# Spacing of the gathers, pieces per step and the distance of the query fold in a two-layer perceiver kernel

## The chip, the cores and the metric

The kernel runs on one core of a Trainium2 chip. The metric is the device time of one execution in microseconds (us). The engines are named as the profile names them: PE multiplies matrices (PEld is its weight load), DVE, ACT and POOL work on vectors, SP issues most of the transfers (DMA). ACT and POOL issue some too.

## What is computed

The input is 16 batches of 64 latent rows of 256 values, in float32, and a context of 16 x 1601 x 256. Two layers follow each other, each with three parts, and each part adds to the latents `x`:

```
x = x + L0_xattn(ctx, ctx, norm(x), mask)   # 16 heads; each query reads 5 places of the context per head
x = x + L0_attn(norm(x))                    # sigmoid attention inside a batch
x = x + L0_ffn(norm(x))                     # 8 experts, the best 2 per row
x = x + L1_xattn(norm(x), ctx)              # 16 heads of 64; 77 text rows and 1524 image rows, two softmaxes
x = x + L1_attn(norm(x))                    # a state space layer
x = x + L1_ffn(norm(x))                     # 32 experts, the best 4 per row, and shared ones
```

In the first cross attention keys and values of all context rows are projected, and each query then reads, for each head and each of five sampling places, two neighbouring rows and weighs them:

```
i0 = floor(ix); w0 = 1 - dx; w1 = dx
sk = 0.5 * (w0 * gather(K, i0) + w1 * gather(K, i0 + 1))      # the same for sv with V
ctx = softmax(Q . sk / sqrt(16)) . sv
```

## The kernel before, in words

The 1024 latent rows are eight tiles of 128 rows (two batches to a tile), kept on the chip in `x4`. PE, DVE and ACT run in an order written out by hand in the code (`manual_schedule`, so their instructions stand as the program issues them). The instructions of POOL and SP are placed by the framework, which may put a load ahead of its place in the code.

**Keys and values** (`keys_values`, lines 364 to 411). A loop over `s` from 0 to 112 makes one step of it each time: seven steps per batch. A step transposes up to two chunks of 128 context rows (`cx`, L153), and projects the chunks of the span before (`st<-wkv,cxt`, L88) into `kv`, which ACT copies out of the accumulators (L382) and writes to a table in memory (`tab<-kv`). `texts` (from step 18) prepares the text part of the second layer's cross attention beside it.

**Gathers and attends.** For each tile and each four heads there is a unit, 32 in all, four per tile. `gather(k)` issues half a unit: a copy of ten columns of indices on DVE (`ig`, L427) and ten indirect transfers on POOL (`g<-tab,ig`, L429); `ig` and `g` have four buffers each. `attend(i)` computes one unit's attention on DVE, in two halves with an exponential on ACT in the first (L449 to L481); it writes `cv`. When these are issued is decided by `tick(us)`, called at many places with a fixed number that stands for the time gone by. It keeps a sum, `now`. A gather is issued at the first call at which `now` has reached `pace["gather"]`, as long as it is less than four units ahead of the attends, and it sets the next time `APART` later, or `APART_X` once cross attention exists (`cr`). A unit's two halves may be issued from `AFTER` (42) on after its last gather. At most one gather and one half are issued in a call. The loop calls `tick(3.9)` in each step from step 0, `tick(2.4)` more while the texts run, and gathers are open from step 14.

**The first tiles' part.** At step 60 the text pools are closed and a pool `lp` is opened for tiles 0 and 1, then tile 2: their attention (`attention`) and dense experts (`middle`, eight experts of four pieces, three weight loads of 512 KB to an expert into four buffers `w`). Tile 3's attention (`late`) goes with them. `mid` issues one piece, if enough units are attended (8 for tiles 0 and 1, 12 for tile 2, 16 for tile 3), and calls `tick(2.4)` for it, and `tick(1.0)` for a piece of `late`:

```
        def mid():

            if mids and attended() >= mids[0][0]:
                if next(mids[0][1], True) is None:
                    tick(2.4)
                else:
                    mids.pop(0)
            if len(mids) < 2 and attended() >= 4 * (ND0 + 1) and next(late, True) is None:
                tick(1.0)
```

What is left of them when the keys and values are done is issued alone, in a loop `while mids`, before cross attention begins.

**Cross attention of the second layer** (`Cross`). `begin` loads text keys and values (`kt`, `vt`), weights (`wk`, `wq`), makes the queries of tile 0, turns the first batch's context (`cn`, `turn`) and folds the first queries. Then 131 steps follow, one for each of 16 batches times 8 pairs of heads, and three to end. Step `n` takes the folded query `qf` of its pair, multiplies it with the context in three groups (`st<-qf,cT`, L88), each in one of four accumulator banks `st`; DVE takes the maximum of each group (`mp`, L1090), PE turns it (L1109), DVE reduces it (`xmx`, L1111), PE spreads it (L1119), ACT copies it (`mc`, L1121). DVE subtracts it from the groups (`pt`, L1130) and ACT takes exponentials. In the same step PE multiplies the `pt` of step n-1 with the context (L1059, three parts), and finishes step n-2 (`turn_out`, `out`). `fold` multiplies the key weights with a query (L1015), and ACT copies the result into `qf` (L1018). A step calls `tick(5.2)` three times.

Steps run without side work until all 32 units are attended. Then a side chain (attention and routed experts of tiles 3 to 7) runs along, up to five pieces a step, as long as the step is below 42; what is left of it is drained alone. Then come three groups of the state space layer and the routing of the last part (`Ssm.group`, `Route.group`); group g begins when step 32 g + 35 is reached and runs on as side pieces of the steps. The last group and the experts of the second layer follow from about 3000 us on.

In `Ssm.group` the normalized rows are the tile `mn`, their transposes `mt`, the product of input and step width `dx`, and the output sum `y` (the tile `ys`), each with one buffer of 128 x 2 x 256 values.

Of the kernel before, what the change touches and what calls it, by code (L numbers as in the profile page):

```python
# [17 lines left out]
P = 128  # L18
B, S, D = 16, 64, 256
M = 1601  # L20
KC = D // P
# [3 lines left out]
NS = H0 * NK  # L25
LEFT = -NK // 2
HU = 4
APART, APART_X, AFTER = 16.0, 12.0, 42.0
RP = 4


# [34 lines left out]
def perceiver_kernel(ctx: ExitStack, tc: tile.TileContext, a: dict, out: bass.AP):  # L66
    nc = tc.nc

    def mk(pool, shape, tag, dtype=F32, bufs=None):
        return pool.tile(list(shape), dtype, tag=tag, name=tag, bufs=bufs)  # L70
# [836 lines left out]
    class Cross:  # L907
# [98 lines left out]
        def fold(self, n):  # L1006

            if n >= B * NHP:
                return
            b, hp = divmod(n, NHP)  # L1010
            w = self.w[b, hp // 4]
            rhs = qbds[b // 2 % 2][:, hp, b % 2].rearrange("p h q -> p (h q)")
            pf = bank()
            for k in range(KC):
                nc.tensor.matmul(pf[:, k * P : (k + 1) * P], lhsT=w[:, hp % 4, k * P : (k + 1) * P], rhs=rhs,  # L1015
                                 start=True, stop=True)
            qf = self.qf[n] = mk(self.xp, [P, KC, P], "qf", bufs=2)
            nc.scalar.copy(qf.rearrange("p c n -> p (c n)"), pf[:, : KC * P])  # L1018

        def out(self, n):  # L1020
# [49 lines left out]
        def step(self, side=None, mid=None, more=None, late=None):  # L1070

            n = self.n
            b, hp = divmod(n, NHP)
            t, bb = divmod(b, 2)
            last = B * NHP
            live = n < last
            old = 0 <= n - 1 < last
            if live:
                ct, qf = self.ctx[b], self.qf.pop(n)
                mp_ = mk(self.xp, [P, NB, P], "mp", bufs=1)  # L1080
                st = []
            for i in range(NB):
                if live:
                    s = big().rearrange("p (c n) -> p c n", n=P)
                    for c in range(4):
                        j = (i * 4 + c) * P
                        mm(s[:, c, :], [(ct[:, k, j : j + P], qf[:, k, :]) for k in range(KC)])
                    st.append(s)
                if live:
                    nc.vector.tensor_reduce(mp_[:, i, :], s.rearrange("p c n -> p n c"), AX.X, ALU.max)  # L1090
                    if i:
                        nc.vector.tensor_tensor(mp_[:, 0, :], mp_[:, 0, :], mp_[:, i, :], ALU.max)
                if i == 1 and n - 2 < last:
                    self.turn_out(n - 2)
                if i == 1 and more is not None:
                    next(more, None)
                if i == 0:
                    tick(5.2)
            if n - 2 < last:
                self.out(n - 2)  # L1100
            if hp == NHP - 1:
                self.turn(b + 1)
            if old:
                po = bank()[:, : D + 1]
                self.product(n - 1, 0, po)
            if live:

                tm = bank()
                nc.tensor.transpose(tm[:, :P], mp_[:, 0, :], ident)  # L1109
                mx = mk(small, [P, 1], "xmx")  # L1110
                nc.vector.tensor_reduce(mx, tm[:, :P], AX.X, ALU.max)  # L1111
            if mid is not None:
                next(mid, None)
            tick(5.2)
            if old:
                self.product(n - 1, 1, po)
            if live:
                mb = bank()
                nc.tensor.transpose(mb[:, :P], mx.to_broadcast([P, P]), ident)  # L1119
                mc = mk(self.xp, [P, P], "mc", bufs=1)  # L1120
                nc.scalar.copy(mc, mb[:, :P])  # L1121
                mc = mc.unsqueeze(1)
            self.fold(n + 1)
            if live:
                pt = pts[n % 2]
                for i in range(NB):
                    c0 = i * 4
                    m = 4 if i + 1 < NB else 3
                    o = pt[:, c0 : c0 + m, :]
                    nc.vector.tensor_tensor(o, st[i][:, :m, :], mc.to_broadcast([P, m, P]), ALU.subtract)  # L1130
                    nc.scalar.activation(o, o, AF.Exp)  # L1131
                o = pt[:CR, CM, :]
                nc.vector.tensor_tensor(o, st[-1][:CR, 3, :], mc[:CR, 0, :], ALU.subtract)
                nc.scalar.activation(o, o, AF.Exp)
            if late is not None:
                next(late, None)
            if old:
                self.product(n - 1, 2, po)
                rc = mk(small, [P, 1], "xrc")
                nc.vector.reciprocal(rc, po[:, D:])  # L1140
                os_ = self.os[n - 1] = mk(self.xp, [P, D], "os", bufs=1)
                nc.vector.tensor_scalar(os_, po[:, :D], rc, None, ALU.mult)

            if hp == 0:
                self.weights(b, 1)
                self.text_loads(b + 1)
            if hp == 1 and b >= 1:
                self.loads(b + 1)
            if hp == 4:
                self.weights(b + 1, 0)  # L1150
            if bb == 1 and hp in (2, 3, 4):
                self.queries(t + 1, hp - 2)
            if hp == 5:
                self.text(b + 1, 0)
            elif hp == 6:
                self.text(b + 1, 1)
                self.text_turn(b + 1, 0)
            elif hp == 7:
                self.text_turn(b + 1, 1)
            if bb == 0 and hp == 2:  # L1160
                self.project(t - 1)
            if side is not None:
                next(side, None)
            tick(5.2)
            self.n += 1

        def begin(self, xp):
            self.xp = xp
            self.text_loads(0)
            self.weights(0, 0)  # L1170
            yield
            for part in range(3):
                self.queries(0, part)
                yield
            self.turn(0)
            self.loads(1)
            yield
            self.text(0, 0)
            yield
            self.text(0, 1)  # L1180
            self.text_turn(0, 0)
            yield
            self.text_turn(0, 1)
            self.fold(0)
            yield


# [4 lines left out]
    class Ssm:  # L1192
# [15 lines left out]
        def group(self, g, wide=None):  # L1208

            mp, w_in, w_xp, w_out, cw, cb, dp, al = (  # L1210
                self.mp, self.w_in, self.w_xp, self.w_out, self.cw, self.cb, self.dp, self.al)
            tiles = range(g * TG, (g + 1) * TG)
            sh = [P, KC, TOK]
# [59 lines left out]
            nc.vector.tensor_scalar(dt, dt, 0.0, None, ALU.max)  # L1273
            nc.vector.scalar_tensor_tensor(dt, q_, 2.0, dt, ALU.mult, ALU.add)
            yield
            dx = mk(mp, sh, "dx")
            y = mk(mp, sh, "ys")
            nc.vector.tensor_tensor(dx, xc, dt.unsqueeze(1).to_broadcast(sh), ALU.mult)
            for c in range(KC):
                nc.vector.tensor_scalar(y[:, c, :], xc[:, c, :], dp[:, c : c + 1], None, ALU.mult)  # L1280
# [223 lines left out]
    cr = None  # L1504
# [6 lines left out]
    def tick(us):  # L1511

        pace["now"] += us
        now = pace["now"]
        k = pace["k"]
        if pace["open"] and now >= pace["gather"] and k < 2 * len(units) and k // 2 < attended() + 4:
            gather(k)
            pace["due"][k // 2] = now + AFTER
            pace["k"] = k + 1
            pace["gather"] = now + (APART if cr is None else APART_X)  # L1520
        i = attended()
        if i < len(units) and pace["k"] > 2 * i + 1 and now >= pace["due"][i]:
            next(attends)
            pace["sub"] += 1

    ET = mybir.EngineType
    with tc.manual_schedule(engines={ET.PE, ET.DVE, ET.Activation}):
# [25 lines left out]
        for s in range(B * 7 + 1):  # L1553
            run(kv)
            if s >= 1:
                run(early)
            if s == 14:
                pace["open"] = True
            tick(3.9)
            if s >= 18 and next(text, True) is None:  # L1560
                tick(2.4)
            if s == 60:
                drain(text)
                stx.close()
                tc.swap_default_side()
                slp = ExitStack()
                lp = slp.enter_context(tc.tile_pool(name="lp", bufs=2))
                tc.swap_default_side()
                mw = Middle(lp)
                for t0, nt in ((0, TG), (TG, ND0 - TG)):  # L1570
                    mids += [(4 * (t0 + nt), attention(t0, nt, lp, mw)), (0, middle(t0, nt, lp, mw))]
                late = attention(ND0, 1, lp, mw)
                for k in range(KC):
                    nc.vector.tensor_scalar(rws[:, k, :], rws[:, k, :], rsc[:, k : k + 1], None, ALU.mult)
            if lp:
                mid()
        drain(kv)
        skv.close()
# [2 lines left out]
        cr = Cross(xc)  # L1581
# [161 lines left out]
```

## Time and profile before

| | us |
|---|---|
| median of 3 runs | 3313.22 (3308.72 to 3315.46) |
| time of the profiled execution | 3307.06 |
| its span, first to last instruction | 3305.1 |
| PE busy in the span | 2924.7 |
| DVE, ACT, POOL busy | 1620.0, 1026.4, 818.2 |
| mean granted clock of PE | 0.946 |

The span is that of the instructions in one profiled execution; 2 us lie around it. An engine is busy while it executes; waiting, branching and issuing of transfers do not count. The clock is the share of full speed that the throttle granted to PE. In the tables of time windows each row has the window and its length, then the busy time of each engine with the number of instructions in brackets, then the clock, the mean busy share of the 16 DMA engines, and what they moved in GB/s. A row of waits names the engine and what it wanted to do, after the arrow what ended the wait, then us in total, the number of waits, and the longest.

### The profile page before, as it was taken

What the parts mean: (1) busy time and instruction counts of PE and PEld (TensorE: products, weight loads), DVE (VectorE), ACT (ScalarE), POOL (GpSimd) and SP (SyncE); (2) the same over time, 40 slices, a digit from 0 to 9 for tenths busy, and PEclk for the clock granted to TensorE, in tenths of its full rate; (3) what the DMA queues carried; (4) which work ended last, traced back from release to release, by engine and by line L of the source; (5) the groups of instructions that cost most, each with busy time, mean ns of one, the idle gap of its engine ahead of it and who ended that gap; (6) DMA issues with size and microseconds to landing.
All of it is one profiled execution on the core that took longest, in us unless ns stands there. A gap on an engine that the chain in (4) does not pass through costs nothing.

```text
span 3305.1 us, 46546 instructions
## 1 busy us (share of the span) xinstructions
PE 2924.7 (88%) x17734; PEld 2402.8 (73%) x17734; DVE 1620.0 (49%) x4143; ACT 1026.4 (31%) x2379; POOL 818.2 (25%) x923
## 2 busy tenths in 40 slices
PE   8779887995678888987997999999999999998879
PEld 4444444564567777876897999989999999896667
DVE  2421113224345445655332577557654487655846
ACT  3233333323212211233242433334323333222421
POOL 0444335545455455200001011001100011000721
PEclk9889998997789899988998999999999999999999
DMA  6387754662511211200454121112210122003884
GB/s 203 102 148 159 239 155 128 180 194 83 154 24 30 58 52 38 75 23 30 137 175 148 44 62 59 50 45 71 66 34 30 57 66 63 26 1 115 257 239 123
DMA packets 339015, 326.06 MB, mean 99 GB/s; under 512 B 59349, under 2 KB 289017, under 8 KB 338281
## 3 DMA queue, kind: packets, MB, share of 16 engines
q1 hardware_dynamic: 186297, 225.11, 22.9%
q10 hardware_dynamic: 126928, 63.06, 7.0%
q0 software_dynamic: 25568, 34.91, 4.9%
q8 instruction: 141, 2.31, 0.3%
q14 instruction: 81, 0.66, 0.1%
HBM read 248.37 MB, written 74.62 MB: 98 GB/s over the span
## 4 chain that ended last, share of the span: by engine, by line
PE 74%; DVE 10%; another core or an unknown queue 5%; issue 4%; DMA 3%; ACT 3%; POOL 0%; SPq 0%; DVEq 0%; ACTq 0%; POOLq 0%
PE st L88 31%; PE mm L1059 19%; PE mm L88 15%; PE mm L153 5%; PE mm L1015 2%; DMA wg<-in_guT 1%; PE mm L1045 1%; DVE hs L1298 1%; DVE mp L1090 1%; PE mm L984 1%; DVE pt L1130 1%; DMA w<-in_gate 1%; PE mm L1109 1%; DVE hc L1303 0%
## 5 line engine op out<-in xcount | busy, mean ns | idle before, releaser
L88 PE MATMUL st<-qf,cT 128*128 128x128 f32 x6144 | 761.3, 282 | 42.2 <-ACT qf L1018 31.9
L429 POOL DMA_INDIRECT g<-tab,ig x640 | 616.2, 963 | 720.8 <-DVE ig L427 519.6
L88 PEld LDWEIGHTS st<-qf,cT 128*128 128x128 f32 x6144 | 739.8, 198 | 52.4 <-ACT qf L1018 35.6
L1059 PE MATMUL mm<-cn,pt 128*128 128x257 f32 (+1 forms) x3072 | 755.8, 390 | 2.0 <-DVE cT L84 1.2
L1059 PEld LDWEIGHTS mm<-cn,pt 128*128 128x128 f32 (+1 forms) x3072 | 563.8, 193 | 88.0 <-DVE cT L84 2.0
L88 PE MATMUL st<-wkv,cxt 128*128 128x512 f32 (+1 forms) x832 | 401.4, 629 | 53.7 <-ACT kv L382 28.7
L1090 DVE TENSOR_REDUCE mp<-st 128x128 f32<-128x512 f32 x384 | 261.1, 688 | 253.5 <-PE st L88 232.6
L88 PEld LDWEIGHTS st<-wkv,cxt 128*128 128x128 f32 (+1 forms) x832 | 157.0, 198 | 226.8 <-issue 178.1
L1130 DVE TENSOR_TENSOR pt<-st,mc 128x512 f32<-128x512 f32 (+1 forms) x384 | 224.2, 640 | 156.5 <-ACT mc L1121 133.9
L1131 ACT ACTIVATE pt<-pt 128x512 f32<-128x512 f32 (+1 forms) x384 | 207.3, 588 | 57.6 <-DVE pt L1130 51.2
L382 ACT COPY kv<-st 128x512 f32<-128x512 f32 (+1 forms) x208 | 118.9, 591 | 234.1 <-PE st L88 128.7
L1121 ACT COPY mc<-mm 128x128 f32<-128x128 f32 x128 | 33.9, 265 | 464.8 <-PE mm L1119 328.4
L1111 DVE TENSOR_REDUCE xmx<-mm 128x1 f32<-128x128 f32 x128 | 37.3, 292 | 229.3 <-PE mm L1109 180.1
L1068 ACT COPY ot<-mm 128x256 f32<-128x256 f32 x128 | 47.2, 369 | 294.8 <-PE mm L153 294.7
L920 POOL MEMSET cn<- 128x12 f32 x16 | 1.8, 119 | 544.5 <-PE mm L1059 520.3
L461 DVE TENSOR_REDUCE smx<-sc 128x4 f32<-128x20 f32 x32 | 5.4, 168 | 244.5 <-ACT sc L459 233.9
L1304 POOL TENSOR_TENSOR ys<-ys,hc 128x512 f32<-128x512 f32 x64 | 81.5, 1273 | 161.2 <-DVE hc L1303 160.9
L1388 POOL DMA_INDIRECT xb<-xnd,row x55 | 55.2, 1004 | 262.9 <-PE mm L1045 221.6
L88 PE MATMUL mm<-xt,w 128*128 128x256 f32 (+1 forms) x512 | 103.0, 359 | 14.3 <-issue 8.4
L88 PEld LDWEIGHTS mm<-xt,w 128*128 128x128 f32 x512 | 89.6, 218 | 31.0 <-issue 21.2
L1035 ACT COPY yt<-mm 128x64 f32<-128x64 f32 x128 | 27.2, 212 | 252.7 <-PE mm L88 230.6
L153 PEld LDWEIGHTS mm<-ident,cx 128*128 128x128 f32 (+1 forms) x416 | 54.9, 150 | 44.4 <-issue 31.7
(455 smaller groups left out, 3994.5 us busy)
## 6 DMA issues: line engine op xcount, KB each, us to landing
tab<-kv ACTq DMA_DIRECT2D x48, 1024.0 KB
w<-in_gate SPq DMA_DIRECT2D x66, 512.0 KB
cx<-in_ctx SPq DMA_DIRECT2D x48, 512.0 KB
cn<-in_ctx SPq DMA_DIRECT2D x16, 1408.0 KB
wg<-in_guT SPq DMA_DIRECT2D x87, 256.0 KB
w<-in_lin SPq DMA_DIRECT2D x33, 512.0 KB
wk<-in_xwkiT SPq DMA_DIRECT2D x32, 512.0 KB
wd<-in_down1T SPq DMA_DIRECT2D x87, 128.0 KB
```

Source lines behind the costliest of these rows:

```text
L88: nc.tensor.matmul(o, lhsT=l, rhs=r, start=i == 0, stop=i == len(pairs) - 1)
L153: nc.tensor.transpose(t[:ncol, i, :rows], b, ident[:rows, :rows])
L382: nc.scalar.copy(kv[:w, :, c, :], pk[:w].rearrange("p (h e) -> p h e", h=H0))
L429: nc.gpsimd.indirect_dma_start(out=gf[:, (half * n + s) * 4 * HD0 : (half * n + s + 1) * 4 * HD0], out_offset=None, in_=tables[j], in_offs ...
L1015: nc.tensor.matmul(pf[:, k * P : (k + 1) * P], lhsT=w[:, hp % 4, k * P : (k + 1) * P], rhs=rhs, start=True, stop=True)
L1059: nc.tensor.matmul(po, lhsT=pt[:w, c, :], rhs=cn[:w, c, :], start=c == 0, stop=c == NCH - 1)
L1068: nc.scalar.copy(ot, tp[:, :KC, :])
L1090: nc.vector.tensor_reduce(mp_[:, i, :], s.rearrange("p c n -> p n c"), AX.X, ALU.max)
L1130: nc.vector.tensor_tensor(o, st[i][:, :m, :], mc.to_broadcast([P, m, P]), ALU.subtract)
L1131: nc.scalar.activation(o, o, AF.Exp)
L1304: nc.gpsimd.tensor_tensor(y, y, hc, ALU.add)
L1388: nc.gpsimd.indirect_dma_start(out=x, out_offset=None, in_=xnd, in_offset=bass.IndirectOffsetOnAxis(ap=tb.row[:, i : i + 1], axis=0))
```

## The change

`APART_X` is dropped and `APART` becomes 12 from 16, so that gathers are 12 apart in `tick`'s time before cross attention as well as in it. From step 60 on the loop over keys and values calls `mid` twice in each step. In cross attention `fold` is called for step n+2 in step n, not for n+1; `qf` has three buffers, and `begin` folds the first two. `dx` and `y` of the state space layer are given the tiles `mt` and `mn`, which frees two tiles.

```
-APART, APART_X, AFTER = 16.0, 12.0, 42.0
+APART, AFTER = 12.0, 42.0
@@ fold
-            qf = self.qf[n] = mk(self.xp, [P, KC, P], "qf", bufs=2)
+            qf = self.qf[n] = mk(self.xp, [P, KC, P], "qf", bufs=3)
@@ step
-            self.fold(n + 1)
+            self.fold(n + 2)
@@ begin
             self.text_turn(0, 1)
             self.fold(0)
+            self.fold(1)
             yield
@@ group of the state space layer
-            dx = mk(mp, sh, "dx")
-            y = mk(mp, sh, "ys")
+            dx = mk(mp, sh, "mt")
+            y = mk(mp, sh, "mn")
@@ tick
-            pace["gather"] = now + (APART if cr is None else APART_X)
+            pace["gather"] = now + APART
@@ loop over keys and values
             if lp:
+                mid()
                 mid()
```

## The prediction, made before the changed kernel ran

> **What bounds the kernel now.** I read the page first, for which engine sets the time and where it doesn't.
>
> ```profile
> span 3305.1 us, 46546 instructions
> PE 2924.7 (88%) x17734; PEld 2402.8 (73%) x17734; DVE 1620.0 (49%) x4143; ACT 1026.4 (31%) x2379; POOL 818.2 (25%) x923
> PE   8779887995678888987997999999999999998879
> PEclk9889998997789899988998999999999999999999
> ```
>
> PE bounds the span: its idle time is 380 us in all. The slices show where that lies: digits 5 and 6 in the tenth and eleventh slice, 7 and 8 up to the eighteenth, then 9 for 1200 us. So no instruction's price is the question; it is how much idle PE time, and how much time at a lowered clock, the new order removes. I cut the span at its stages (keys and values to step 60, with and without the first tiles' pieces; those pieces alone; the start of cross attention; cross attention with attends; with the side work; with the state space layer).
>
> ```profile
> core 0: us, PE busy (x) PEld busy (x) DVE busy (x) ACT busy (x) POOL busy (x), PEclk, DMA share, GB/s
> 0.00:402.00 402.00, 332.72 (x1027) 176.01 (x1028) 106.66 (x360) 128.49 (x253) 144.71 (x163) 0.92 0.68 168
> 402.00:482.00 80.00, 67.37 (x195) 31.74 (x194) 6.29 (x19) 26.97 (x50) 35.09 (x37) 0.94 0.63 174
> 482.00:715.00 233.00, 204.41 (x713) 122.90 (x711) 72.85 (x232) 90.62 (x170) 114.80 (x122) 0.95 0.56 156
> 715.00:879.00 164.00, 110.14 (x500) 91.00 (x501) 63.32 (x201) 42.89 (x84) 86.11 (x90) 0.78 0.45 132
> 879.00:912.00 33.00, 18.81 (x115) 16.80 (x113) 9.88 (x26) 10.53 (x23) 9.44 (x10) 0.75 0.48 144
> 912.00:1180.00 268.00, 211.32 (x1400) 188.84 (x1401) 132.91 (x338) 51.21 (x137) 140.85 (x146) 0.90 0.15 36
> 1180.00:1403.00 223.00, 189.29 (x1300) 169.00 (x1298) 122.80 (x311) 47.61 (x132) 93.15 (x103) 0.95 0.21 58
> 1403.00:1764.00 361.00, 320.63 (x2207) 291.87 (x2208) 158.70 (x484) 125.05 (x277) 16.32 (x19) 0.94 0.33 103
> 1764.00:1812.00 48.00, 31.22 (x220) 28.16 (x220) 12.46 (x29) 9.87 (x22) 10.40 (x16) 0.88 0.35 105
> 1812.00:3001.00 1189.00, 1180.87 (x8768) 1083.86 (x8766) 744.34 (x1670) 408.25 (x994) 67.80 (x108) 1.00 0.16 47
> ```
>
> The poorest stage is 715 to 879: tiles 0 to 2's attention and dense experts alone, 54 us idle and the clock at 0.78. It exists because these pieces wait for `attended()`, which waits for gathers. Next are the two rows of cross attention with attends (27 steps, 912 to 1403): 90 us idle. In the last row a step has no idle time at all: steps 83 to 98 (2388.4 to 2604.8 by the starts of the `xmx` reductions) take 13.5 us each, against 491/27 = 18.2 here. Third, the waits: whole trace first (engine, line, what it waited for; total us, times, longest), then PE's in 912 to 1180 and in 715 to 912.
>
> ```profile
> POOL g L429 <- DVE ig L427: 519.6, 48, 87.1
> POOL g L429 <- issue: 174.4, 568, 1.1
> ```
>
> ```profile
> PE st L88 <- ACT qf L1018: 16.8, 6, 4.6
> PE mm L1109 <- DVE mp L1092: 15.3, 2, 13.4
> ```
>
> ```profile
> PE mm L153 <- DVE vb L477: 9.4, 1, 9.4
> ```
>
> POOL idles for the order to gather, not for data; a scheduled spacing, not POOL, paces the gathers. PE waits for `qf` only where attends run, and for a finished attend in 715 to 912.
>
> **The order, part by part.** I followed `tick` through the code. Before, gathers stand 15 to 19.5 ticks apart until step 112; attend 7 ends at step 77, the first piece of tiles 0 and 1 is issued there, and 36 of about 92 pieces are placed when step 112 ends. With 12 they stand 12.6 to 13.5 apart: attend 7 ends at step 55, pieces start at step 60 (where their pool opens), two a step, and all, the late tile's too, are placed by about step 108. Cross attention then begins with 7 attends left, not 14, and so runs 14 steps with attends, not 27; the side work starts at step 14 and ends of itself at step 32 instead of being cut off at 42 and drained. The number of cross steps, 131, is the same.
>
> **1. Keys and values, to 402 us (step 60):** two more attends and six more gathers beside PE, which is 83% busy where DVE is 27%. 0 us; without that cover, two attends of some 6.3 us of DVE work, 13 us.
>
> **2. Steps 60 to 112.** PE work: 67.4 + 204.4 = 271.8 us in 313 us (87% busy), plus the 110.1 us that stood alone. Those ran at clock 0.78; at the 0.95 of their new neighbours they are 110.1 x 0.78/0.95 = 90. Sum 362. How full can PE be? The longer steps give the `tab` writes more time, which helps; two pieces in one step sometimes wait for each other (query layer norm, then its transposes), which hurts. I take 89%: 362/0.89 = 407, so the stage ends at 809 where the pieces ended at 879: **-70**. At 95% it is -96, at 83% -41. DMA is no worse: 48 steps carry some 34 MB of context and tables and 25 MB of expert weights in about 385 us, 153 GB/s, like the 156 of the row 482 to 715. The 48 weight loads stand on SP's queue among the context loads; a load placed for a new expert waits until the expert two before is finished, now 1.5 steps ahead (about 13 us), not 3. The first 512 KB context load held the chain for 9.6 us, so 13 should do; where it doesn't, the expert's first matmul is late by a few us each, which the 83% allows for. ACT gets five more loads of function tables (1.28 us each in the chain), covered by PE; without that, 6.4 us.
>
> **3. Start of cross attention.** `cn` of batch 0 was loaded under the 164 us stage. Now its space is free only when the last `kv` copy is written out: estimate 10 us (a `tab` write held the chain for 14.9 at 377) and 8 for 1.4 MB. On SP the loads of `kt`, `vt`, `wk`, `wq` now stand ahead of it and are no longer waited for (6 us of the chain at 885). The query matmuls cover most. 35 us instead of 33, between 28 and 45: **+2**.
>
> **4. Cross steps with attends.** 14 steps with 7 attends took 268 us in 912 to 1180. `qf` folded two ahead takes away the 16.8 us wait, but the next thing PE meets is its second score group, whose bank is freed by the `pt` subtraction, which stands behind the second half of the attend on DVE. So I count half, -8 (between 0 and -17). Step 0 no longer has an attend; of its 13.4 us wait for `mp` I count -5 (0 to -13), since its releaser isn't named. 255. **-13**.
>
> **5. The 13 steps that lose their attends or gathers** took 223 us (1180 to 1403). Placed elsewhere without them they cost their PE work: 189.3 x 0.95 = 180 (13 x 13.5 = 176 by the other route). **-43**. The added `fold` distance costs nothing here: the same matmuls and copies one step earlier, weights loaded 1.5 steps (20 us) ahead instead of 2.5, PE never idle in those rows; if that cover went, 32 loads of half a MB would each show a few us.
>
> **6. Side work.** 361 + 48 us; the last 48, a drain with no step beside it, held 16.8 us idle. Now three of the 13 steps fill it: **-15** (-5 to -17).
>
> **7. `dx` and `y` in the tiles of `mt` and `mn`:** their readers (projection, transposes) are many steps done, the next writer needs `y`'s result in any case. 0; the cover is the chain of the layer itself, and PE's cross steps beside it; without them a wait on DVE holds `decay` up behind it, by the 0.4 us of a turned copy in each of four groups.
>
> **8. POOL.** A gather group is 10 x (0.957 + 0.307) = 12.6 us (row 715 to 879: 86.11/90; issue: 174.4/568). From about step 83, with one tile's short pieces, ticks run ahead of the clock, 213 ticks in some 180 us: a group each 11.3 us. Over 16 groups POOL falls 20 us behind; the 42 ticks between gather and attend leave about 21. **+5** (0 to 25).
>
> Here a rule speaks against the change: the Trainium skill, "SBUF — State Buffer", section "SBUF: two separate sides", says a DMA issued by GpSimd needs descriptors that GpSimd cannot write while a VectorE operation in a two-port mode holds their shared port. The rows: DVE 25, 39 and 50% busy in 83 to 402, 715 to 879 and 912 to 1180, gathers there 959, 957 and 971 ns. By the row DVE at about 50% costs 15 ns a gather, nothing. By the rule, if a gather met half of an 0.83 us `pr` half the time (estimate: +0.2 us), a group would be 14.6, the 53 groups from 94 us would end at 868, and the sum lose 59 us. I go by the row.
>
> The moved 110 us also rests on the clock: the same skill, "TensorE: Matmul & The Clock Gate", section "Part 1: The HAM clock gate (the “warmup” mystery)", knows half and full clock only, full after 3.4 us busy. Were PE warm throughout, the 362 would be 344 and the stage 20 us shorter; the rows with pieces between steps show 0.95, so I keep that.
>
> **Sum:** -70 + 2 - 13 - 43 - 15 + 5 = -134. The profiled execution took 3307.1 us, so 3173. The median of the runs shown is 3313.2, 6.2 more: **3179**.
>
> **Rivals.** A, *the pieces bring their gaps along*: the 54 us idle of 715 to 879 are waits inside the pieces (9.4 for `vb`, then `att`, `act`, weights), and two a step leave less between them to hide them than one. Then item 2 is 313 + 90 + 54 = 457, ends at 859 and brings 20 instead of 70. For: each pair of adjoining pieces of an attention depends on itself through DVE and ACT. Against: the 36 pieces already placed went in at 88%, and the largest of those waits, for an attend, can't come again, as attends are now ahead. 3229.
> B, *gathers bound the stage*: place, POOL, steps 18 to 112; price, per gather g. 53 groups from 94 us: the stage ends no earlier than 94 + 530 g. That decides from g = 1.35 us, and eats the whole gain at an end of 809 + 134 = 943, g = 1.60. Measured 1.26. At 1.70, a gather blocked for half a `pr` every time, it ends at 995: 3179 - 5 + 186 = 3360, slower than before. For: the `ig` copy of a group waits for the group four before, so DVE, and with it ACT and PE, would be held too. Against: the 15 ns above.
> C, *the later part doesn't come*: PE in the moved steps isn't free of gaps, they go with other work (turns, projections, side pieces), so 5 and 6 bring half: 3208. For: the digits of the side work are 7 to 9 too. Against: from 1812 on there is no idle time with side work on every step.
>
> **Numbers.** Forecast 0.68, C 0.13, A 0.13, B or a slip of such a size 0.06. The forecast alone: 3140 to 3220 (items 2, 3, 4, 8 at their ends, not all at once). The range, with A and C, 3125 to 3238. A measurement of this kernel tells 0.2%, 6.6 us, from no change: faster 0.91, same 0.02, slower 0.07.
>
> **What would show it.** Right: no stretch with PE clock under 0.85 between step 112 and cross attention; the last `tab` write near 805 and the first score matmul near 845; 14 attend steps in about 255 us; `qf` gone from PE's waits there; the last cross steps as before at 12.3 us. Wrong: `g` releasing `pr` on DVE, or POOL with no wait for `ig` (B); PE under 85% busy from 402 on, with `kv`, `w` or `act` as releaser (A); PE idle in the side work (C).

## The result: slower, and by how much depends on the chip

| | before | changed | ratio |
|---|---|---|---|
| median | 3316.48 (3307.07 to 3338.99) | 3349.88 (3328.39 to 3365.46) | 1.0093 [1.0073, 1.0112] |
| profiled execution | 3307.06 | 3349.21 | |
| its span | 3305.1 | 3347.5 | |

The forecast was 3179. The medians are over 18 runs each. The page of the changed kernel has as much PE work as before, at a lower mean clock (0.935, before 0.946), and more idle slices ahead of cross attention:

```profile
span 3347.5 us, 46678 instructions
PE 2923.4 (87%) x17734; PEld 2396.7 (72%) x17734; DVE 1621.0 (48%) x4143; ACT 1032.9 (31%) x2384; POOL 819.7 (24%) x923
PE   8758867866666888879999999999999999998879
PEclk9878988987877989989999999999999999999989
```

Cut at the stages (to step 60; steps 60 to 112 with the pieces; the start of cross attention; its 14 steps with attends; the side work and what follows it):

```profile
core 0: us, PE busy (x) PEld busy (x) DVE busy (x) ACT busy (x) POOL busy (x), PEclk, DMA share, GB/s
0.00:458.00 458.00, 342.03 (x1032) 180.43 (x1032) 120.33 (x399) 126.53 (x253) 205.51 (x229) 0.87 0.62 153
458.00:1013.00 555.00, 396.17 (x1426) 252.63 (x1426) 171.19 (x541) 166.06 (x318) 312.08 (x320) 0.83 0.46 131
1013.00:1048.00 35.00, 21.92 (x140) 19.94 (x139) 14.13 (x36) 11.62 (x23) 3.33 (x6) 0.80 0.58 165
1048.00:1289.00 241.00, 202.03 (x1349) 181.05 (x1350) 127.31 (x325) 52.98 (x138) 103.41 (x113) 0.90 0.17 47
1289.00:1620.00 331.00, 289.89 (x1965) 261.30 (x1965) 149.79 (x466) 110.89 (x250) 13.51 (x16) 0.92 0.30 95
```

The order is the forecast one: pieces from step 60 on, two a step, all placed before step 112 ends, then 14 steps with attends and the side work from step 14 on. But step 60 comes at 458 us (before: 400), and steps 60 to 112 last 555 us, in which PE is 71% busy (396.17/555) at a clock of 0.83. Cross attention's first `xmx` comes at 1047.9 us, 126 later than before (921.8). From there to the end the changed kernel wins 84 us (2383.3 before, 2299.6 now), so 42 are lost.

**What PE waits for.** The chain of waits in the stage of keys and values (100 us to the stage's end), shares by line, first of the kernel before, then of the changed one:

```profile
by line: PE st L88 34.4%; PE mm L88 24.1%; another core or an unknown queue 13.1%; issue 6.8%; PE mm L153 5.4%; DMA tab<-kv 1.9%; DMA w<-in_gate 1.7%; ACT kv L382 1.5%; DVE cv L473 0.8%; POOL g L429 0.6%; DVE pr L471 0.5%; ACT L833 0.5%; PE
by line: PE mm L88 22.2%; PE st L88 21.6%; another core or an unknown queue 20.5%; issue 14.2%; PE mm L153 4.6%; POOL g L429 2.0%; ACT kv L382 2.0%; DMA cx<-in_ctx 0.6%; DVE pr L449 0.6%; DMA g<-tab,ig 0.6%; DMA tab<-kv 0.6%; DVE s L451 0.5
```

A core that runs alone waits for no other core. "Unknown" and "issue" together are 20% of the chain before and 35% after. The waits of the changed kernel from 100 to 1013 us show where the unknown stands (`remote` is the same thing: nothing in the trace released it at that time):

```profile
POOL g L429 <- DVE ig L427: 235.7, 26, 27.2
ACT kv L382 <- remote: 88.0, 17, 9.2
DVE qp L311 <- remote: 53.0, 2, 27.1
ACT gl L833 <- remote: 50.8, 9, 20.1
ACT cxt L398 <- remote: 42.8, 8, 10.3
DVE x L814 <- remote: 42.8, 5, 14.3
```

All five readers take what PE has written. One such place in the changed kernel, by the timeline (start, length, what; in brackets the idle time before and its releaser), PE first, then ACT, then POOL:

```profile
770.61 8.01 PE L88 MATMUL st<-wkv,cxt 128*128 128x512 f32 x16
778.45 0.38 PE L153 MATMUL mm<-ident,xn 128*128 128x128 f32 x2
778.67 0.38 PE L153 MATMUL mm<-ident,zn 128*128 128x128 f32 x2
795.83 1.02 PE L88 MATMUL mm<-rws,xt 128*128 128x8 f32 x4 [16.77 <-ACT xt L173]
```

```profile
780.76 0.27 ACT L398 COPY cxt<-mm 128x130 f32<-128x130 f32 x1 [4.07 <-remote]
789.89 0.59 ACT L382 COPY kv<-st 128x512 f32<-128x512 f32 x1 [8.86 <-remote]
793.40 1.56 ACT L382 COPY kv<-st 128x512 f32<-128x512 f32 x3 [2.92 <-remote]
```

```profile
750.89 0.94 POOL L429 DMA_INDIRECT g<-tab,ig  x1 [5.98 <-DVE ig L427]
752.13 0.94 POOL L429 DMA_INDIRECT g<-tab,ig  x1 [0.30 <-issue]
...
787.67 0.94 POOL L429 DMA_INDIRECT g<-tab,ig  x1 [0.30 <-issue]
802.79 0.94 POOL L429 DMA_INDIRECT g<-tab,ig  x1 [14.17 <-DVE ig L427]
```

The 8.01 us of matmuls fill four `st`, and the first is ready at 773.5 by its recorded end. ACT, idle, copies it at 789.89 and the other three from 793.40. PE waits 16.8 us. Meanwhile POOL issues 30 indirect gathers without a break (750.89 to 788.61; `...` stands for rows left out); here the last results come through 4.8 us after the last of them. Over the whole trace, of the `kv` copies that ACT was idle for, those whose matmul ended while gathers ran (or within 1 us of one) started 3.3 us after it on average (up to 23.3), the others 0.04. Before the change the same two numbers are 2.4 and 0.3. So the effect was already there before; the change makes it larger.

Two more readings of the traces tell what is late. A semaphore is a counter by which one engine tells another that it is done, and the trace records its updates. First, are the updates late, or PE's work? In the place above, PE's updates for the second, third and fourth `st` are recorded at 793.38, 793.44 and 793.50, 0.06 us apart, though each stands for four matmuls, and the groups start 1.72 us apart. From 100 to 1013 us, 103 of PE's 410 recorded updates come less than 0.1 us after the one before; in the same program on a chip without the effect (below), 0 of 711 between the same times do. So the matmuls were done one after another, earlier, and the news of it was held up and then passed on in bursts. ACT began 0.02 us after the updates at 789.87 and 793.38, so it was not ACT that was late.

Second, is it only PE's news? In that other trace it can be read off what ended each wait. Of 179 waits of ACT and DVE that PE ended there, 25 ended more than 1.5 us late on the first chip (up to 12.7 us). Of 126 waits that ACT or DVE ended, six did, and all six instructions wait for a semaphore of PE as well. So the delay is in PE's news alone.

### The profile page after: what moved, and what is told of

Read it like the earlier page. It is cut to its first block, busy times and chain, and to the rows that moved or that the text cites. A ratio compares the mean times of both kernels' runs of the same rounds, so it can differ in the third digit from the quotient of the medians.

```text
span 3347.5 us, 46678 instructions
## 1 busy us (share of the span) xinstructions
PE 2923.4 (87%) x17734; PEld 2396.7 (72%) x17734; DVE 1621.0 (48%) x4143; ACT 1032.9 (31%) x2384; POOL 819.7 (24%) x923
## 3 DMA queue, kind: packets, MB, share of 16 engines
q0 software_dynamic: 25568, 34.91, 4.7%
## 4 chain that ended last, share of the span: by engine, by line
PE 71%; DVE 10%; another core or an unknown queue 6%; issue 6%; ACT 3%; DMA 2%; POOL 1%; SPq 0%; ACTq 0%; DVEq 0%
PE st L88 28%; PE mm L1059 19%; PE mm L88 15%; PE mm L153 5%; PE mm L1015 2%; DVE hs L1299 1%; DMA wg<-in_guT 1%; PE mm L1045 1%; PE mm L984 1%; ACT kv L382 1%; POOL g L429 1%; DVE mp L1090 1%; DVE pt L1130 1%; PE mm L1109 0%
## 5 line engine op out<-in xcount | busy, mean ns | idle before, releaser
L88 PE MATMUL st<-qf,cT 128*128 128x128 f32 x6144 | 753.6, 280 | 19.1 <-issue 16.4
L88 PEld LDWEIGHTS st<-qf,cT 128*128 128x128 f32 x6144 | 731.9, 196 | 26.1 <-issue 19.7
L1059 PE MATMUL mm<-cn,pt 128*128 128x257 f32 (+1 forms) x3072 | 746.0, 386 | 2.7 <-issue 2.2
L1305 POOL TENSOR_TENSOR mn<-mn,hc 128x512 f32<-128x512 f32 x64 | 81.6, 1275 | 163.7 <-DVE hc L1304 155.5
L398 ACT COPY cxt<-mm 128x512 f32<-128x512 f32 (+1 forms) x112 | 60.7, 543 | 117.7 <-remote 42.8
```

Source lines behind the costliest of these rows:

```text
L88: nc.tensor.matmul(o, lhsT=l, rhs=r, start=i == 0, stop=i == len(pairs) - 1)
L398: nc.scalar.copy(cxt[:, 2 * q : 2 * q + m, :, :w].rearrange("p r k n -> p (r k) n"), tp[:, : KC * m, :w])
L1059: nc.tensor.matmul(po, lhsT=pt[:w, c, :], rhs=cn[:w, c, :], start=c == 0, stop=c == NCH - 1)
L1305: nc.gpsimd.tensor_tensor(y, y, hc, ALU.add)
```

## The experiments

Theory S: indirect gathers close behind each other make PE's results known late. Rival T: two pieces in one step wait for each other or for weights. The edits are shown shortened; `...` stands for what is left out.

The kernel before did not take the same time on every chip. On chips 10, 4, 7 and 1 its median was 3064 to 3066 us, on chips 6, 9, 15 and 2 it was 3304 to 3321, as beside the first run of the change. I call them quick and late chips. Every ratio is to the kernel before on the same chip.

| experiment | chip | time | ratio |
|---|---|---|---|
| spacing undone | quick | 3061.75 | 0.9991 [0.9981, 1.0000] |
| spacing alone | quick | 3039.9 | 0.9921 [0.9907, 0.9935] |
| two pieces alone | quick | 3062.92 | 0.9991 [0.9982, 1.0001] |
| fold and shared tiles alone | quick | 3062.13 | 0.9994 [0.9986, 1.0002] |
| changed kernel again | quick | 3034.77 | 0.9912 [0.9897, 0.9926] |
| spacing undone, again | quick | 3060.39 | 0.9989 [0.9980, 0.9998] |
| changed, no gathers | quick | 3019.58 | 0.9862 [0.9848, 0.9876] |
| before, no gathers | quick | 3055.14 | 0.9970 [0.9959, 0.9981] |
| groups of five | late | 3376.55 | 1.0235 [1.0193, 1.0276] |
| plain loads | late | 3022.38 | 0.9154 [0.9120, 0.9188] |
| spacing undone | late | 3285.26 | 0.9886 [0.9863, 0.9909] |
| spacing alone | late | 3364.1 | 1.0134 [1.0107, 1.0161] |
| a fill after each gather | quick | 3534.07 | 1.1532 [1.1512, 1.1551] |
| two plain loads | quick | 3139.37 | 1.0246 [1.0225, 1.0266] |
| 20 ticks apart | quick | 3151.74 | 1.0275 [1.0255, 1.0295] |
| two plain loads | late | 3139.28 | 0.9500 [0.9442, 0.9557] |
| indices in order | late | 3346.08 | 1.0084 [1.0058, 1.0109] |
| a fill after each gather | quick | 3537.32 | 1.1533 [1.1509, 1.1557] |

**The parts, one by one.** The changed kernel with the old spacing:

```
-APART, AFTER = 12.0, 42.0
+APART, APART_X, AFTER = 16.0, 12.0, 42.0
-            pace["gather"] = now + APART
+            pace["gather"] = now + (APART if cr is None else APART_X)
```

> The changed kernel with the old spacing (16 before cross attention, 12 in it); two pieces a step and the longer fold distance stay. Theory S (gathers issued back to back on POOL make PE's results known late to ACT and DVE, so closer gathers stall the keys and values): the stall goes, about 3260 to 3300 us, and the keys and values end with no more waits of kv copies on PE than in the kernel before. Rival T (two pieces in a step wait for each other and for their weights): stays near 3340.

The kernel before with `APART` 12 and nothing else:

> The kernel before with the spacing of 12 before cross attention as its only edit. Theory S: slower than before by as much as the whole change or more, 3340 to 3390 us, first cross step near 1000 to 1050 us. Rival T: pieces start at step 60, one a step, and more of them find room: faster, 3230 to 3280.

The kernel before with the second `mid()` in the loop and nothing else:

> The kernel before with two pieces a step as its only edit. Theory S: gathers as before, so some 25 more pieces go beside keys and values: 3260 to 3300 us. Rival T: slower than before, 3330 to 3350.

The kernel before with `fold(n + 2)`, three `qf` and the shared tiles and nothing else:

> The kernel before with the fold two pairs ahead (three qf buffers, dx and y in the tiles mt and mn) as its only edit. Both theories: the wait of score matmuls for qf (32 us in 27 steps) goes in part, 3295 to 3312 us; a result over 3320 would mean that the fold distance or the shared tiles cost something themselves.

Both theories miss: these runs fell on a quick chip, and there the spacing alone wins 0.8% and the other two parts, each alone, are at or inside the bound of 0.1%. In these traces no result of PE is late, although with the spacing alone one run of gathers is 480 long. Two rows of the kernel with only the fold changed (up to cross attention it is the kernel before) on that chip:

```profile
350.00:610.00 260.00, 252.51 (x874) 144.52 (x873) 73.75 (x237) 114.00 (x214) 145.41 (x153) 0.99 0.65 187
798.00:982.00 184.00, 181.17 (x1347) 166.91 (x1348) 126.32 (x323) 52.09 (x136) 134.98 (x142) 0.99 0.21 55
```

Steps 60 to 112 with PE 97% busy, and 14 cross steps beside attends in 184 us; the first trace of the kernel before had 87% and 258 us. Most of the idle time that the prediction meant to remove is not there.

**The whole change on a quick chip, and without gathers.** Without them, POOL fills each half of `g` with a constant:

```
-            nc.gpsimd.indirect_dma_start(out=gf[...], in_=tables[j], in_offset=...)   # ten of these
+        nc.gpsimd.memset(gf[:, half * n * 4 * HD0 : (half + 1) * n * 4 * HD0], 0.25)
```

> The changed kernel once more, beside the kernel before on the same chip. The kernel before took 3316 us beside the first run of the change and 3064 us beside the four parts, and in the second case no result of TensorE reached ScalarE or VectorE late while gathers ran. Theory S (gathers that run back to back make TensorE's results known late, and only where the kernel before takes about 3300 us) expects: where the kernel before takes about 3316 us, a ratio near 1.009, with gl, kv and mc up to 20 us behind their matmuls; where it takes about 3064 us, no such lags, and the sum of the parts' own ratios as the least gain (0.9921 for the spacing alone, 3040 us) with the two pieces and the fold on top: some 3000 us, ratio 0.975 to 0.985. Rival T (two pieces in one step wait for each other, whatever the chip) expects a ratio over 1.00 on either.

> The changed kernel with the old spacing of the gathers (16 and 12 ticks), again, to stand beside the changed kernel in the same call. Theory S: where the kernel before takes about 3316 us, near the kernel before (0.99 to 1.00) while the changed kernel is at 1.009, so that the difference is the spacing; where it takes about 3064 us, 0.999 as measured, and then the changed kernel is faster than this one. Rival T: equal to the changed kernel.

> The changed kernel without its indirect gathers: POOL fills each half gf with a constant, so attention sees other keys; everything else is issued as before. Theory S: where the kernel before takes about 3316 us, TensorE stays near 90 % busy to cross attention, the first xmx comes near 850 us instead of 1048, and the time falls to about 3150 us (0.95); where it takes 3064 us, little is left to win beside the changed kernel itself (under 1 %), unless POOL's gathers bound the stage there (then up to 2 %). Rival T: the first xmx stays where the changed kernel has it.

> The kernel before without its indirect gathers (each half of gf filled with a constant by POOL). Theory S: where the kernel before takes about 3316 us, it wins what the late signals cost there, first xmx near 850 to 870 us instead of 922 and about 3240 us in all; where it takes 3064 us, the gathers cost nothing that shows at the old spacing: within 0.3 % of the kernel before.

Again a quick chip. The changed kernel is faster there, though not by the 0.975 to 0.985 of S: it has the spacing's own gain and nothing on top. T, which expected a loss on either kind of chip, falls here. Stage by stage, steps 60 to 112 and the 14 cross steps of the changed kernel:

```profile
360.00:756.00 396.00, 358.86 (x1433) 232.89 (x1432) 171.84 (x541) 168.10 (x316) 293.34 (x306) 0.96 0.63 184
793.00:977.00 184.00, 180.44 (x1351) 165.48 (x1352) 126.85 (x325) 54.02 (x138) 103.13 (x113) 1.00 0.21 61
```

The same instructions as in the row 458 to 1013 above, with PE 91% busy instead of 71%. The gathers cost the changed kernel 15 us here (3034.8 against 3019.6) and the kernel before 9.

**Smaller groups, and plain loads.** Groups of five, 6.5 ticks apart; and, in the changed kernel, plain loads of the same shape from POOL's queue:

```
+            pace["gather"] = max(pace["gather"], now - 6.5) + 6.5     # n = HU * NK // 4, k counts quarters
```

```
-            nc.gpsimd.indirect_dma_start(out=gf[...], in_=tables[j], in_offset=...)
+            nc.gpsimd.dma_start(out=gf[...], in_=tables[j][s * P : (s + 1) * P, :])
```

> The changed kernel with its gathers in groups of five, 6.5 ticks apart, instead of ten, about 13 apart: the same rate in smaller pieces. Theory S (long runs of gathers on POOL make TensorE's results known late, where the kernel before takes about 3316 us): there, shorter runs as long as no groups are released together, lags under 5 us, the first xmx under 1000 us, ratio 0.97 to 1.00; where the kernel before takes about 3064 us, within 0.3 % of the changed kernel's 0.991, since no result was late there. A rival, that only the sum of the gathers in the stage counts: the same as the changed kernel on either (1.009 or 0.991).

> The changed kernel with each indirect gather replaced by a plain load from POOL's queue, as large (128 rows of a table in order), so attention sees other keys. The changed kernel took 0.9912 of the kernel before, without gathers 0.9862. If what they cost is POOL's time for an indirect one (957 ns each, 640 of them), the plain ones should be shorter on POOL and the ratio near 0.986; if it is the transfers or the waits for them, it stays near 0.991. Theory S where the kernel before takes about 3316 us: late results as with gathers if it is the issuing of transfers by POOL that matters (1.00 to 1.01), none if it is their indirection (0.95 to 0.96).

Now a late chip. With plain loads the kernel takes 3022 us, as on a quick chip without gathers, where the kernel before takes 3304: so what a late chip loses in the changed kernel (3350 us in the first run, 3035 on a quick chip) goes with the indirect gathers. The plain loads use the same queue and are as many packets as the gathers (25568 on it in both kernels). The chain of this run from 100 us to the end of step 112 has no unknown share:

```profile
by line: PE st L88 40.4%; PE mm L88 31.4%; PE mm L153 5.6%; DMA tab<-kv 4.6%; DMA g<-tab 1.6%; issue 1.4%; ACT kv L382 1.3%; ACT L831 0.8%; DVE x L812 0.7%; DVE cv L471 0.6%; ACTq L385 0.6%; DVE pr L469 0.5%; DVE s L449 0.5%; DVE pr L447 0.
```

Groups of five made it worse, which S had not expected: POOL's runs were again 20 gathers long in 14 of 47 cases and 25 or 30 in four more. A late result holds back DVE's `ig` copies, and then several groups are released together.

**The spacing on a late chip.**

> The changed kernel with the old spacing of the gathers (16 and 12 ticks), for the case that the kernel before takes some 3300 us here, as it did beside the first run of the change and beside the groups of five. Theory S then: the indirect gathers stall the stage in both kernels and the closer spacing makes it worse, so that with the old spacing the two pieces and the fold are left, ratio 0.98 to 1.00, first xmx near 910 to 930 us; late results (kv behind its matmuls by 5 us and more) as often as in the kernel before. Rival T (the two pieces lose the time): 1.005 to 1.015, as the whole change. Where the kernel before takes about 3064 us: 0.999 once more.

> The kernel before with the closer spacing alone (12 ticks ahead of cross attention). Where the kernel before takes some 3300 us, theory S: slower, 1.00 to 1.02, first xmx 980 to 1060 us, more of the stage with kv, gl and cxt behind TensorE. Rival T: faster than the kernel before, 0.98 to 0.995, since only the pieces hurt. Where it takes about 3064 us: 0.992 once more.

This settles the step. Spacing 12 alone is slower by 1.3%, everything but the spacing faster by 1.1%, as S said and against T. First `xmx` at 1053.7 and 921.3 us; the `kv` copies are 3.9 and 2.1 us late on average while gathers run. The chains, from 100 us on, of the spacing alone and of the spacing undone:

```profile
by line: PE st L88 26.6%; another core or an unknown queue 21.3%; PE mm L88 18.2%; issue 12.0%; PE mm L153 5.0%; POOL g L429 1.3%; ACT kv L382 1.0%; DVE cv L473 0.7%; DMA g<-tab,ig 0.7%; DVE s L451 0.6%; DVE pr L449 0.6%; DMA cx<-in_ctx 0.6
by line: PE st L88 35.5%; PE mm L88 25.3%; another core or an unknown queue 14.5%; PE mm L153 5.6%; issue 4.4%; DMA tab<-kv 2.1%; ACT kv L382 1.7%; DVE cv L473 0.9%; DMA ktd<-kts 0.7%; DVE pr L471 0.6%; ACT L459 0.5%; ACT cxt L398 0.5%; DVE
```

The shares are those of the two kernels of the first run: 21 and 12% as in the changed one, 15 and 4% near the one before.

**What of the gathers it is.** Changed kernel with a fill of 128x1024 after each gather; with two plain loads in place of a gather; with gathers 20 ticks apart; with indirect gathers whose indices are in order:

```
             nc.gpsimd.indirect_dma_start(...)
+            nc.gpsimd.memset(idle, 0.0)
```

```
+            for _ in range(2): nc.gpsimd.dma_start(out=gf[...], in_=tables[j][s * P : (s + 1) * P, :])
```

```
-APART, AFTER = 12.0, 42.0
+APART, AFTER = 20.0, 42.0
```

```
+        nc.gpsimd.iota(ixo, [[P * 4 * HD0, HU * NK // 2]], base=0, channel_multiplier=4 * HD0)
-        nc.vector.tensor_copy(ig, ix[:, j, c0 : c0 + n])
+        nc.vector.tensor_copy(ig, ixo)
```

> The changed kernel with a fill of about 1 us on POOL after every indirect gather, so that no two gathers touch and a group takes 20 us instead of 10. Where the kernel before takes some 3300 us: if unbroken runs of gathers delay TensorE's results, lags under 3 us and a ratio of 0.93 to 0.98; if each gather costs its share wherever it stands, or if POOL's busy time does it, 1.01 or more. Where the kernel before takes 3064 us: POOL nearer to its limit, 0.995 to 1.01.

> The changed kernel with two plain loads of POOL's queue, 535 ns each, in place of every indirect gather: as long on POOL and twice the bytes; attention sees other keys. Where the kernel before takes some 3300 us: if the indirection makes results late, none are late and the ratio stays near 0.92; if it is POOL issuing transfers for over 12 us on end, lags of 5 to 20 us as with gathers and 1.00 or more. Where the kernel before takes 3064 us: 0.985 to 0.995.

> The changed kernel with gathers 20 ticks apart everywhere. Where the kernel before takes some 3300 us: the spacing of 12 gave 1.009, that of 16 gave 0.989; if the loss follows the density of the gathers, 0.97 to 0.99; if 16 was already loose enough, 0.99 to 1.01, since more attends are left for cross attention (13 us of a step each). Where the kernel before takes 3064 us: 1.00 to 1.02, because later attends hold cross attention's steps back.

> Two plain loads of POOL's queue in place of every indirect gather, again: it took 3139 us where the kernel before takes 3064 us (POOL and the loads bound the stage). Where the kernel before takes some 3300 us: if the indirection makes TensorE's results late, none are late, the time is the same 3139 us and the ratio about 0.95; if it is POOL issuing transfers for over 12 us on end, kv, gl and cxt come 5 to 20 us behind TensorE, and the time is 3300 us or more.

> The changed kernel with its indirect gathers kept and their indices set in order, so that each reads the 128 rows in line that the plain loads read; attention sees other keys. Where the kernel before takes some 3300 us: if the indirect instruction itself makes TensorE's results late, as the changed kernel, 1.00 to 1.02 with kv up to 20 us late; if it is the scattered rows, no late results and about 3030 us, 0.92. Where the kernel before takes 3064 us: as the changed kernel there, 0.985 to 0.995.

> The changed kernel with a fill of 0.96 us on POOL after every gather, again; where the kernel before takes 3064 us it took 3534 us, bound by POOL. Where the kernel before takes some 3300 us: if gathers on end make results late, none are late and the time is again about 3534 us, ratio 1.065 to 1.075; if every gather costs its share wherever it stands, kv comes late as in the changed kernel and the time is over 3600 us.

Two plain loads keep POOL as busy with transfers as a gather does (2 x 535 ns, a gather 963) and take 3139 us on both kinds of chip; on the late one no `kv` copy was late (0.04 us). So it is not POOL issuing transfers for long. (On the quick chip it was slower than I wrote, since the doubled loads waited 245.6 us for each other.) Indirect gathers that read rows in order are as slow as the changed kernel's own (1.0084, and 1.0093 in the first run), with the same mark in the chain (100 to 1010 us):

```profile
by line: PE st L88 27.6%; PE mm L88 23.1%; another core or an unknown queue 19.2%; issue 11.1%; PE mm L153 4.4%; ACT kv L382 1.8%; DMA tab<-kv 1.1%; DVE cv L474 0.7%; DMA ktd<-kts 0.6%; ACTq L385 0.5%; DVE pr L450 0.5%; DVE s L452 0.5%; DVE
```

So it is the indirect instruction, not the scattered rows. Whether it is their runs or their number stays open: both times the fill fell on a quick chip. The first trace speaks for the runs, without proving it: of its 39 `kv` copies that are over 1.5 us late, 36 belong to matmuls that ended 8 us or more after the first gather of an unbroken run. There the fill showed rival B's mechanism instead, POOL as the bound, which I had priced at no more than 1.01. POOL's groups, and the chain from 150 to 1300 us:

```profile
L436 POOL MEMSET idle<- 128x1024 f32 x640 | 611.8, 956 | 30.0
L430 POOL DMA_INDIRECT g<-tab,ig x640 | 608.4, 951 | 198.2 <-issue 173.8 <-DVE ig L428 18.9 <-DMA g<-tab,ig 2.7
by line: POOL g L430 36.7%; POOL idle L436 27.3%; issue 14.1%; DMA g<-tab,ig 4.8%; PE mm L88 3.0%; PE st L88 2.9%; DVE pr L451 0.9%; DVE s L453 0.9%; PE mm L153 0.8%; PE mm L1061 0.7%; ACT L835 0.4%; DVE cv L475 0.4%; DVE smx L465 0.4%; DMA
```

At 951 + 956 ns and 310 of idle time (198.2/640) a gather costs 2.2 us; that costs the changed kernel 499 us (3534 against 3035). Gathers 20 ticks apart also came out slower than I wrote. The last attend then ends beside cross step 43, past step 42, up to which the program leaves room for the first layer of the later tiles; by the program's order part of their queries are then made from unfinished rows, so that kernel's time says only that later attends hold the steps back.

## Why the prediction was wrong

**The step that failed is the second, with the first.** "I take 89%": measured 71% in 458 to 1013, and the stage ended at 1013, not 809. The first, "0 us" to step 60, cost 58. Between them they turn -70 into +134, and the spacing is what does it: with it undone, on a late chip, the first `xmx` is back at 921 us. What these two items had at nothing, and item 8 at +5, is what more gathers beside the keys and values do to others. I priced a gather by its own length (963 ns on average, before and now; going by the row, not by the rule of the Trainium skill, "SBUF — State Buffer", section "SBUF: two separate sides", that VectorE can hold GpSimd's descriptors up, was right) and looked for who waits for it; hardly anyone does. What it delays is the hand-over from PE to ACT and DVE, which no row of a gather shows.

**PE's work was sized right.** 362 us at 89% gives 407; on a quick chip the same steps took 396, with 359 of work. On the first chip the 396 of work there are the same instructions at a clock of 0.83 instead of 0.96. PE idles more often there, and the clock is low where it idles: in the place above it is 1.00 from 775 to 780 us and 0.50 from 785 to 795, while PE stands still.

**The gain before the change was read from the wrong cause.** I put the idle time of cross attention's first 27 steps (18.2 us each) down to the attends beside them. On quick chips 14 steps with attends take 184 us, 13.1 each, and on a late chip with plain loads 182. So the attends are covered on both, and the idle time came with the indirect gathers. That is why the change wins only 29 us on a quick chip. Of the 33 us between the spans of the spacing undone and the changed kernel there, 10 come before the first `xmx` and 23 after it.

**The rest held in size, which was luck in part.** Start and cross attention, on the first chip: from the stage's end to the first `xmx` 34.9 us (42.8 before), the 14 steps from there 17 us shorter (forecast 13), the next 50 steps 66 shorter (forecast 43 + 15), the remainder 0.5. Together -92 where the sum had -69, and +134 - 92 is the +42 of the spans. `qf` is gone from the waits. These steps lose gathers together with their attends, so the saving came on this chip though I had named the wrong cause; on a quick chip the part behind the first `xmx` wins the 23 us above.

**The rivals.** A is not it: PE is under 85% busy from step 60 on, as A said, but of its 159 us of idle time in steps 60 to 112 it waits 14.9 for `act`, 3.3 for `kv` and none for `w`, and the two pieces without the spacing are part of the faster kernel. B is not it for the change: POOL waited 235.7 us for `ig` on the first chip, and on a quick chip, where it waits 22.1, gathers are 2% of the chain. C fell, 66 of 58 us came. None of them, nor the range, held a delay that sits in the trace as an unnamed releaser. It was in the trace of before, for instance (the first three in 100 to 879 us, the last in 912 to 960):

```profile
ACT kv L382 <- remote: 50.8, 14, 7.8
ACT cxt L398 <- remote: 17.1, 3, 11.3
ACT gl L833 <- remote: 15.5, 3, 5.5
DVE mp L1090 <- remote: 15.9, 2, 9.8
```

I had passed over the first three as not being PE's. They belong to the 13.1% of the chain that the closer gathers would raise. The last stands behind the 13.4 us wait for `mp` in item 4, "since its releaser isn't named": there the sign was noticed and not followed.

## What to carry to other kernels

When a one-core trace names "another core or an unknown queue" as a releaser, find out what runs beside those waits before pricing a change that brings more of it. Idle time is put down to a cause only when the same work is seen without that cause. And a kernel tuned around such an effect is tuned for a chip: on a late chip the change without its spacing (0.9886) beats both kernels, on a quick one the whole change (0.9912) does, and with no indirect gathers both kinds run alike (3020 us with constants on a quick one, 3022 with plain loads on a late one).

## What the runs showed of the hardware

On the chip of the first run, whose number is not on record, and on three of the eight numbered ones (6, 9, 2), news of PE's results reaches ACT and DVE up to 27 us late (the longest, in the groups of five) while POOL issues indirect gathers on end. A fourth, 15, is late by the time of the kernel before (3312 us); its one trace has plain loads. Mostly it begins some ten microseconds into a run of gathers (the 36 of 39 above). Of 173 `kv` copies over 3 us late in the six such traces, 101 came through while gathers still ran, 68 within about 5 us after the last. In the traces of the other four chips no news of PE comes late (on chip 1 only the kernel with the fill was traced; on chip 10 one run is 480 gathers long). Plain loads from the same queue don't do it.

Why chips differ is not known here: each chip has one set of runs, so the chip, the hour and whatever else ran on it can't be told apart, and the late ones also scatter more (3281 to 3324 us for the kernel before on one, 3059 to 3071 on a quick one). One more thing marks the late chips. In their traces part of the semaphore records is missing: 410 of PE's 487 are there from 100 to 1013 us of the changed kernel, on the quick chip all but one of 712. Some are missing in the last 400 us too, with plain loads as well, where no wait is put down to `remote`. Every time here comes from an execution that was recorded, so whether the recording has a part in the delay stays open; no run tests it.
